# Attention A's output projection as seven block products for each pair of token tiles

## The chip, the cores and the metric

The kernel runs on one core of one Trainium2 chip. The metric is the device time of one execution in microseconds (us), as the median of several runs. All times of single instructions come from one profiled execution of the kernel before the change.

## The reference, cut to what matters

The program is one block of a transformer on an input of 2 sequences (B = 2) of T = 1024 tokens of C = 1024 features, all float32: attention A (32 heads of 32, causal, with ten adapter tokens), a feed-forward layer, attention B, and the same feed-forward layer again, each with a residual. The change concerns the last line of attention A and its residual:

```
y = einsum('bhqk,bhkd->bhqd', softmax(q k / sqrt(32), causal), v)
y = y + gating * einsum('bhqk,xhkd->bhqd', softmax(q ak / sqrt(C)), av)
y = y.transpose(0, 2, 1, 3).reshape(B, T, C)
x = x + einsum('btc,oc->bto', y, w_proj)
```

The last line is the output projection: a product of 2048 x 1024 by 1024 x 1024. Everything after it reads this x.

## The kernel before, in words

**Order of the work.** TensorE's (PE's) instructions are issued in program order. Attention A works in half-steps (`attend`, L454 to L533). In each of them PE multiplies scores twice: "s" scores (`sc`), from which VectorE (DVE) takes the row minimum (`pr_A`, `nmax_A`, L332), and transposed "t" scores (`st`), which ScalarE (ACT) turns into weights (`pt`, L503), and which then multiply the values (`y_A`, L413). Between the half-steps the `Filler` (L49 to L144) issues dense work from a queue of generators: the q, k and v projections of later heads, then the output projection. `fill.run` (L531) issues as much of it as an estimate of 1.7 ns for each column allows (`FILL_A`, L37); `fill.drain` issues what is left. `fill.chore` puts small DVE work in a list, one piece of which is issued after each fill step, and `fill.flush(key)` issues all pieces up to the last one with this key.

**Matmuls.** `mm` (L204) issues a product of a 128x128 block (`lhsT`, the stationary operand) and 128x512 columns (`rhs`) as one call at L207, or, directly behind attention's own matmuls, as four calls of 32 columns of the block each at L209. In float32 each call becomes two instructions in the trace. So one such product is 2 records at L207 or 8 at L209.

**The projections of q, k and v** (`seven`, L651) already use seven products of blocks in place of eight, in the form of Winograd. `factors` (L643) makes the combinations of the left blocks as chores, `combine` (L622) those of the right blocks, which go through DRAM and come back as `tt` tiles. The products land in two PSUM banks by turns, tags `ca` and `cb` (`block_bank`, L163), and DVE adds them up (L670 to L689).

**The output projection** (`proj_a`, L1020) is a plain product. For each of the 8 token tiles of a sequence, `yt` (128 features x 8 groups x 128 tokens) is fetched by eight DMAs of 64 KB from `yd`, where attention left its result. For each half of the 1024 output columns, eight products of 128x128 by 128x512 accumulate in one bank `op` (L1055), DVE adds the residual from `xp` (L1062), and SyncE's queue (SP) stores the sum to `x1` (L1063). So a tile takes 16 products, and a sequence 128. The weights `wp` are two tiles of 16 KB a partition (L1040) in the places of the normalized input.

Sequence 0's projection (`proj_a(0)`, L1009) is the last fill of attention A; what attention leaves of it is drained at L1304. Then the PSUM pool `psA` is closed, a new one with three `ps` banks is opened (L1306), and sequence 1's projection (`proj_a(1)`, L1310) runs with nothing beside it. It also issues the loads of the later weights (`each`, three in each tile). It is followed by the first feed-forward layer (`f1`), whose first tile is fetched and normalized within the last two tiles of the projection (`then.prepare`, L1049).

**SBUF.** Pool `big` holds `h16` (2 x 16 KB a partition: normalized input, later `wp`), `t4k` (3 x 4 KB: `yt`), `tt` (5 x 2 KB: `xp`). Pool `wkA` holds attention A's own tiles, among them the weights `wqk` (2 x 8 KB) and `wv` (8 KB); it is closed before the drain at L1304, and the later stages' weights take its place. In stage A the DMAs of SP are ordered by a scheduler; from L1308 on they go in program order.

**The adapter tokens.** For each group g of four heads of sequence 0, `adapter_parts` multiplies the adapter's tokens by the weights (L787), and `adapter_keys` (L792) and `adapter_values` (L798) sum the parts some fill steps later (L896, L929, L951). They share the only bank of tag `ps` with `shift_rows` and `adapter_scores`. `begin(b, g)` (L817) issues the parts and the left factors of the next group, for every group at the end of the previous one's projection (L838).

## Time and profile before

| what | value |
|---|---|
| time, median of 3 runs (lowest, highest) | 2494.17 us (2489.88, 2497.11) |
| the profiled execution | 2490.82 us, of which its span in the profile is 2489.1 us |
| output projection of sequence 0, between attention A's steps | 1205.8 to 1350 us |
| the rest of it and sequence 1's, alone on PE | 1350 to 1492 us |
| records of its matmuls | 338 at L207 and 696 at L209 |

Times inside an execution are counted from the start of the span. "Busy" is the time in which an engine worked on an instruction; matmuls overlap in their pipeline, so their durations add up to more than the time that they take, and the time from start to start is the better measure. "Idle before, releaser" names what an engine waited for before an instruction. SP's rows are the issuing of DMAs; a long SP row includes the time that SP waited for the tile to be ready or free.

### The profile page before, as it was taken

The numbers are of one execution on the slowest core, as the hardware profiler recorded it, in microseconds if no ns is written. First come the engines' busy times: TensorE is split into PE (matmuls) and PEld (weight loads), VectorE is DVE, ScalarE is ACT, GpSimd is POOL, SyncE is SP. The second block draws the span as 40 slices with busy tenths as digits, with TensorE's granted clock in tenths as the row PEclk, the third lists the DMA queues.
The fourth block names the chain that finished last, engine by engine and source line by source line (L and its number), as shares of the span: only waits on it lengthen the run. The fifth ranks groups of instructions, "written<-read, shape, count | busy, mean of one in ns | idle before, by whom it ended". The sixth has DMA issues, their size and how long they took to land.

```text
span 2489.1 us, 60414 instructions
## 1 busy us (share of the span) xinstructions
PE 2433.3 (98%) x25477; PEld 1101.6 (44%) x25477; DVE 1339.2 (54%) x4120; ACT 1090.0 (44%) x2085; POOL 499.1 (20%) x800
## 2 busy tenths in 40 slices
PE   7899999999999999999999999999999999999999
PEld 4434444455444545444433445574333653333344
DVE  7665665665656666665510114366554765654243
ACT  3346665665655666666631000012354535555200
POOL 1332322232423323322100001101000101111120
PEclk9999999999999999999999999999999999999999
DMA  6632322333333333333222541130110310212121
GB/s 214 208 90 80 104 86 84 100 90 103 125 93 104 93 105 95 91 90 117 86 69 81 190 158 64 43 102 26 41 37 27 137 35 35 86 43 94 40 97 42
DMA packets 142512, 224.34 MB, mean 90 GB/s; under 512 B 12832, under 2 KB 73376, under 8 KB 142240
## 3 DMA queue, kind: packets, MB, share of 16 engines
q1 hardware_dynamic: 142240, 220.48, 27.6%
q8 instruction: 199, 3.26, 0.5%
q14 instruction: 73, 0.60, 0.1%
HBM read 168.01 MB, written 52.43 MB: 89 GB/s over the span
## 4 chain that ended last, share of the span: by engine, by line
PE 88%; DVE 6%; issue 2%; DMA 2%; ACT 1%; POOL 1%; SPq 0%; DVEq 0%; ACTq 0%; POOLq 0%
PE fo_f L207 11%; PE st L391 9%; PE fo_f L209 7%; PE sc L319 7%; PE op L207 6%; PE y_A L413 5%; PE y L209 5%; PE z L209 3%; PE st L389 3%; PE op L209 3%; PE y_v L209 3%; PE x L209 3%; PE y_B L413 2%; PE bq L207 2%; DVE pr_A L332 2%
## 5 line engine op out<-in xcount | busy, mean ns | idle before, releaser
L503 ACT ACTIVATE pt<-st 128x1024 f32<-128x1024 f32 (+1 forms) x418 | 426.0, 1019 | 654.5 <-PE st L391 490.6
L340 ACT ACTIVATE pr_A<-pr_A,nmax_A 128x896 f32<-128x896 f32 (+7 forms) x512 | 389.9, 765 | 47.2 <-DVE nmax_A L332 46.5
L332 DVE CUSTOM_DVE_ANT_0 pr_A<-sc,mask 128x512 f32<-128x512 f32 (+3 forms) x512 | 251.1, 537 | 200.0 <-PE st L391 103.5
L319 PE MATMUL sc<-kT,qT 32*128 32x512 f32 (+3 forms) x1536 | 329.1, 525 | 4.4 <-DVE nmax_A L332 3.6
L391 PE MATMUL st<-qT,kT 32*128 32x512 f32 (+3 forms) x1536 | 307.2, 487 | 0.0
L207 PE MATMUL fo_f<-wb,xt_f 128*128 128x512 f32 x558 | 253.0, 596 | 0.4 <-ACT hwT_f L1153 0.4
L236 POOL TENSOR_TENSOR xf<-xf,b_base 128x256 f32<-128x256 f32 x128 | 89.3, 729 | 761.0 <-DVE xn_f L258 457.2
L332 DVE CUSTOM_DVE_ANT_0 pr_A<-sc,mask,part_A 128x512 f32<-128x512 f32 (+1 forms) x256 | 156.2, 647 | 147.3 <-PE sc L319 98.7
L209 PE MATMUL fo_f<-wb,xt_f 128*32 128x512 f32 x1864 | 223.6, 599 | 0.0
L398 POOL TENSOR_SCALAR_AFFINE_SELECT pt<-pt 128x256 f32<-128x256 f32 x256 | 104.5, 426 | 525.3 <-ACT pt L503 525.3
L340 ACT ACTIVATE pr_B<-pr_B,nmax_B 128x1024 f32<-128x1024 f32 x128 | 145.6, 1140 | 41.2 <-DVE nmax_B L332 41.2
L413 PE MATMUL y_A<-pt,v 128*32 128x512 f32 (+3 forms) x1536 | 157.9, 498 | 0.0
L207 PEld LDWEIGHTS fo_f<-wb,xt_f 128*128 128x128 f32 x558 | 103.4, 193 | 113.9 <-issue 113.3
L319 PE MATMUL sc<-kq,qk 32*128 32x512 f32 x512 | 144.3, 640 | 3.7 <-DVE nmax_B L332 3.3
L207 PE MATMUL op<-wp,yt 128*128 128x512 f32 x338 | 145.7, 592 | 0.0
L391 PE MATMUL st<-rows_B,kq 32*128 32x512 f32 x512 | 144.3, 640 | 0.0
L250 ACT ACTIVATE lv_f<-ve_f 128x1 f32<-128x1 f32 x32 | 6.5, 203 | 309.9 <-DVE ve_f L248 309.9
L391 PEld LDWEIGHTS st<-qT,kT 32*128 32x128 f32 x1536 | 134.0, 185 | 16.5 <-issue 11.4
L332 DVE CUSTOM_DVE_ANT_0 pr_B<-sc,mask,part_B 128x512 f32<-128x512 f32 x128 | 91.2, 747 | 79.8 <-PE sc L319 79.7
L389 PE MATMUL st<-rows_A,ones 3*128 3x512 bf16 (+3 forms) x768 | 127.8, 329 | 4.1 <-DVE nmax_A L332 4.1
L332 DVE CUSTOM_DVE_ANT_0 pr_B<-sc,mask 128x512 f32<-128x512 f32 x128 | 83.4, 687 | 75.9 <-PE sc L319 75.9
L319 PEld LDWEIGHTS sc<-kT,qT 32*128 32x128 f32 x1536 | 113.5, 184 | 18.6 <-issue 9.2
(274 smaller groups left out, 3648.2 us busy)
## 6 DMA issues: line engine op xcount, KB each, us to landing
tt<-td SPq DMA_DIRECT2D x252, 256.0 KB, 2.8
wqk<-in_w_attnT SPq DMA_DIRECT2D x32, 512.0 KB, 5.2
xf<-x SPq DMA_DIRECT2D x32, 512.0 KB, 3.3
xa<-in_x SPq DMA_DIRECT2D x16, 512.0 KB, 6.1
wv<-in_w_attnT SPq DMA_DIRECT2D x8, 1024.0 KB, 5.3
yd<-ys SPq DMA_DIRECT2D x32, 256.0 KB, 2.9
yt<-yd SPq DMA_DIRECT2D x128, 64.0 KB, 2.0
xp<-in_x SPq DMA_DIRECT2D x32, 256.0 KB, 2.9
```

Source lines behind the costliest of these rows:

```text
L207: return pe.matmul(out, lhsT=lhsT, rhs=rhs, start=start, stop=stop, skip_group_check=True)
L209: pe.matmul(out[i : i + 32], lhsT=lhsT[:, i : i + 32], rhs=rhs, start=start, stop=stop, skip_group_check=True)
L236: pool.tensor_add(dst[:, i : i + 2 * P], a[:, i : i + 2 * P], b[:, i : i + 2 * P])
L250: act.activation(lv, ve, AF.Ln)
L319: yield w * COL, lambda: pe.matmul(dst[:, o : o + w], lhsT=self.qt[rows, qc : qc + P], rhs=self.kt[rows, c0 : c0 + w], start=True, stop=True)
L332: minimum[0] = dve.tensor_tensor_reduce(pr[:, c0 : c0 + w], sc[:, i, o : o + w], m, -self.scale, BIG if c0 == 0 else self.part[:, col], AL ...
L340: tc.keep_in_program_order(act.activation(pr[:, :nk], pr[:, :nk], AF.Exp, bias=self.nmax[:, col], scale=-1.0, accum_out=self.sums[:, col]))
L389: yield w * COL / 4, lambda: pe.matmul(dst[:, o : o + w], lhsT=ones[three, :], rhs=self.rows[three, off : off + w], start=True, stop=False)
L391: yield w * COL, lambda: pe.matmul(dst[:, o : o + w], lhsT=self.kt[rows, kb * P : (kb + 1) * P], rhs=rhs, start=self.extra, stop=True)
L398: pool.affine_select(out=dg, in_=dg, compare_op=ALU.is_ge, fill=0.0, base=0, pattern=[[0, 2], [1, P]], channel_multiplier=-1)
L413: pe.matmul(self.y[32 * h : 32 * h + 32, off : off + w], lhsT=self.value(h, kb), rhs=pt[h // 2][:, h % 2, o : o + w], start=self.opens, st ...
L503: act.activation(pt[:, :, low_:wide_], st[:, :, low_:wide_], AF.Exp, scale=ts[0][0].scale)
```

## The change

Sequence by sequence, two token tiles form a pair. A pair's product is 256 tokens x 1024 by 1024 x 1024, seen as a 2x2 matrix of blocks (128 tokens x 512) times a 2x2 matrix of blocks (512 x 512). A plain product needs eight products of blocks, each of four matmuls (128x128 by 128x512). The change forms it from seven (`seven_added`), with sums and differences of blocks made by DVE (`left_factors` for the left, chores for the right). Pair 0 of sequence 0 is still computed plainly, while the three combinations of the weights are made; these lie in the places of `wqk` and `wv`, for which the two tags move to pool `big`. The last difference (`b12 - b11`) is made in place behind pair 0.

For this, sequence 0's projection is drained inside the pool `wkA`, in whose places (`sa`, `sv`, `qr`) the left factors and the sums lie, and sequence 1's projection runs in the PSUM pool of attention A, in the banks `ca` and `cb`, with a new small SBUF pool `pj`; the PSUM pool is exchanged behind it. A pair's `yt` tiles are fetched at the start of the pair before, its `xp` tiles behind the second product of the pair before, and each store is issued one addition late.

Three more things move in stage A: `begin(b, 1)` goes from the end of group 0's projection to the middle of it, ahead of `combine`; `adapter_keys` goes from fill step 4 to 12; and `adapter_values` from step 4 to 8, and for group 0 from the first pair of tiles to the second.

The diff, cut to its core:

```
         def v_load(b, g):
-            wv = wk.tile([P, NC, 2 * P], F32, tag="wv", name=f"wv{b}_{g}", bufs=1)
+            wv = big.tile([P, NC, 2 * P], F32, tag="wv", name=f"wv{b}_{g}", bufs=1)
...
-            if ng and nb < B:
+            if g and ng and nb < B:
                 yield from begin(nb, ng)
...
                     if b == 0:
                         yield from between
+                    yield from begin(b, 1)
                     combine(b)
...
-                    if i == 4 and b == 0:
+                    if i == 12 and b == 0:
                         yield adapter_keys(g)
...
-                    if i == 4 and b == 0 and g == e:
+                    if i == 8 and b == 0 and g == e:
                         yield adapter_values(g)
...
-                if n == 0 and t == 0:
+                if n == 0 and t == 2:
                     yield adapter_values(0)
...
+        def place(kind, i, shape, name):
+            if kind == "yt" or kind == "x":
+                return big.tile(shape, F32, tag={"yt": "t4k", "x": "tt"}[kind], name=name)
+            return wk.tile(shape, F32, tag={"s": "sa", "sum": ("sv", "sv", "qr")[i]}[kind], name=name, bufs=2)
+
+        fill.add(Dense(lambda: proj_a(0, big, wp, place)))
...
+    def seven_added(nm, left, right, ready, sums, x, ended):
+        s1, s2, s3 = sums
+        def product(i, dst, start=True, stop=True):
+            ready(i)
+            for k in range(4):
+                mm(dst, lhsT=left[i][:, k, :], rhs=right[i][:, k, :], start=start and k == 0, stop=stop and k == 3)
+                yield HF * COL
+        def added(i, s):
+            pin_add(x[i], s, x[i])
+            ended(i)
+        first = block_bank([P, HF], f"x_{nm}")
+        yield from product(1, first, stop=False)
+        act.copy(s1, first)
+        y = block_bank([P, HF], f"y6_{nm}", 1)
+        yield from product(6, y)
+        pin_add(s2, s1, y)
+        yield from product(2, first, start=False)
+        added(11, first)
+        y = block_bank([P, HF], f"y7_{nm}", 1)
+        yield from product(7, y)
+        pin_add(s1, s2, y)
+        pin_sub(left[3], left[3], left[6])
+        z = block_bank([P, HF], f"z_{nm}")
+        yield from product(5, z, stop=False)
+        pin_add(s3, s1, z)
+        added(22, s3)
+        y = block_bank([P, HF], f"y4_{nm}", 1)
+        yield from product(4, y)
+        pin_sub(s1, s1, y)
+        added(21, s1)
+        yield from product(3, z, start=False)
+        pin_add(s2, s2, z)
+        added(12, s2)
+        pair.rotate(1)
+
+    def left_factors(a, s1, s2, key):
+        for op, dst, x, y in ((pin_add, s1, a[21], a[22]), (pin_sub, s2, s1, a[11]), (pin_sub, a[21], a[11], a[21])):
+            fill.chore(key, lambda op=op, dst=dst, x=x, y=y: op(dst, x, y))
+        return {1: a[11], 2: a[12], 3: a[12], 4: a[22], 5: s1, 6: s2, 7: a[21]}
+
+    def proj_a(b, big, wp, tile_of, then=None, each=None):
...
+        def fetch(p):
+            for t in (2 * p + 1, 2 * p):
+                yts[t] = take("yt", [P, NG, P], f"yt{b}_{t}")
+                for g in range(NG):
+                    sp.dma_start(yts[t][:, g, :], yd[b, g][:, t * P : (t + 1) * P])
...
+        def store(t, n):
+            stores.append((x1[b, t][:, n * HF : (n + 1) * HF], xs.pop((t, n))))
+            if len(stores) > 1:
+                sp.dma_start(*stores.popleft())
...
+            for i, tag in ((3, "wqk"), (2, "wqk"), (4, "wv")):
+                wp["T", i] = big.tile([P, 4, HF], F32, tag=tag, name=f"wpt{i}")
...
+        for p in range(NT // 2):
+            if then is not None and p == NT // 2 - 1:
+                then.prepare()
+            if p + 1 < NT // 2:
+                fetch(p + 1)
+            if each is not None:
+                each()
+            if b == 0 and p == 0:
+                for c in range(4):
+                    for dst, op, x, y in ((7, pin_sub, b22, b12), (6, pin_add, right[7], b11), (4, pin_sub, right[6], b21)):
+                        fill.chore("wp", lambda c=c, dst=dst, op=op, x=x, y=y: op(right[dst][:, c], x[:, c], y[:, c]))
...
+                for c in range(4):
+                    fill.chore("wp1", lambda c=c: pin_sub(b12[:, c], b12[:, c], b11[:, c]))
+                continue
...
+            flush = {6: ("wp", nm), 5: ("wp1",)}
...
+            def ready(i):
+                for key in flush.get(i, ()):
+                    fill.flush(key)
+                if i == 2:
+                    while stores:
+                        sp.dma_start(*stores.popleft())
+                    if p + 1 < NT // 2:
+                        fetch_x(p + 1)
+                if i == 5:
+                    if each is not None:
+                        each()
+                    if then is not None and p == NT // 2 - 1:
+                        then.prepare()
...
-            big = PoolOf(bigp, {"h16": 2, "t4k": 3, "tt": RING})
+            big = PoolOf(bigp, {"h16": 2, "t4k": 3, "tt": RING, "wqk": 2, "wv": 1})
...
-            fill.drain()
-            psa.close()
-            ps = ctx.enter_context(tc.tile_pool(name="ps", bufs=3, space=bass.MemoryType.PSUM, reuse_waits="tile"))
+                fill.drain()
...
+            pj = PoolOf(own.enter_context(tc.tile_pool(name="pj", bufs=2, side="right", reuse_waits="tile")), {"sum": 3, "x": 3, "yt": 1})
...
+            fill.add(Dense(lambda: proj_a(1, big, wp, place, f1_0, lambda: load(3))))
             fill.drain()
             assert not loads
+            own.close()
+            psa.close()
+            ps = ctx.enter_context(tc.tile_pool(name="ps", bufs=3, space=bass.MemoryType.PSUM, reuse_waits="tile"))
```

More of the change, by code (lines that the diff above doesn't have):

```diff
@@ L224, in pin, with in_pieces, both, pin_sub @@
         return r
+    def in_pieces(op):
+        def both(dst, x, y):
+            for h in range(0, HF, 2 * P):
+                op(dst[:, h : h + 2 * P], x[:, h : h + 2 * P], y[:, h : h + 2 * P])
+        return both
+    def pin_sub(*a):
+        pin(dve.tensor_sub(*a))
+    def pin_add(*a):
+        pin(dve.tensor_add(*a))
     def evac(dst, src):
@@ L603, in stage_a @@
         streams = {}
-        def in_pieces(op):
-            def both(dst, x, y):
-                for h in range(0, HF, 2 * P):
-                    op(dst[:, h : h + 2 * P], x[:, h : h + 2 * P], y[:, h : h + 2 * P])
-            return both
-        def pin_sub(*a):
-            pin(dve.tensor_sub(*a))
-        def pin_add(*a):
-            pin(dve.tensor_add(*a))
         def made(ts, b, i, c, op, x, y):
@@ L703, in qk_load @@
         def qk_load(b, g):
-            wqk = wk.tile([P, NC, 2, P], F32, tag="wqk", name=f"wqk{b}_{g}", bufs=2)
+            wqk = big.tile([P, NC, 2, P], F32, tag="wqk", name=f"wqk{b}_{g}", bufs=2)
             for s in range(2):
@@ L1007, in stage_a @@
                          ("unit", f"A{old // NG}_{old % NG}_1") if old >= 0 else None)
-        wp = []
-        fill.add(Dense(lambda: proj_a(0, big, wp)))
+        wp = {}
+        def place(kind, i, shape, name):
[3 more added lines that the diff above has]
+        fill.add(Dense(lambda: proj_a(0, big, wp, place)))
         attend([make(b, g, n) for b in range(B) for g in range(NG) for n in range(2)], FILL_A, late)
@@ L1017, in ahead_of @@
                 yield r
-    def proj_a(b, big, wp, then=None, each=None):
-        yts, xs = {}, {}
-        def fetch(t):
-            if t >= NT:
-                return
-            yts[t] = big.tile([P, NG, P], F32, tag="t4k", name=f"yt{b}_{t}")
-            for g in range(NG):
-                sp.dma_start(yts[t][:, g, :], yd[b, g][:, t * P : (t + 1) * P])
-        def fetch_x(t):
-            if t >= NT:
-                return
-            for n in range(2):
-                xs[t, n] = big.tile([P, HF], F32, tag="tt", name=f"xp{b}_{t}_{n}")
+    def seven_added(nm, left, right, ready, sums, x, ended):
[32 more added lines that the diff above has]
+        pair.rotate(1)
@@ new lines, in left_factors, with take, fetch_x @@
+    def left_factors(a, s1, s2, key):
[3 more added lines that the diff above has]
+    def proj_a(b, big, wp, tile_of, then=None, each=None):
+        yts, xs, stores = {}, {}, deque()
+        count = {"yt": 0, "x": 0}
+        def take(kind, shape, name):
+            count[kind] += 1
+            return tile_of(kind, count[kind] - 1, shape, name)
+        def fetch(p):
[3 more added lines that the diff above has]
+                    sp.dma_start(yts[t][:, g, :], yd[b, g][:, t * P : (t + 1) * P])
+        def fetch_x(p):
+            for t, n in ((2 * p, 0), (2 * p + 1, 1), (2 * p + 1, 0), (2 * p, 1)):
+                xs[t, n] = take("x", [P, HF], f"xp{b}_{t}_{n}")
@@ L1036, in fetch_x @@
                 sp.dma_start(xs[t, n], d["x"][b, t * P : (t + 1) * P, n * HF : (n + 1) * HF])
+        def store(t, n):
+            stores.append((x1[b, t][:, n * HF : (n + 1) * HF], xs.pop((t, n))))
+            if len(stores) > 1:
+                sp.dma_start(*stores.popleft())
         if not wp:
             for i in range(2):
-                wp.append(big.tile([P, 4, C], F32, tag="h16", name=f"wp{i}"))
+                wp[i] = big.tile([P, 4, C], F32, tag="h16", name=f"wp{i}")
                 for g in range(4):
@@ L1042, in proj_a @@
                     sp.dma_start(wp[i][:, g, :], d["w_projT"][(4 * i + g) * P : (4 * i + g + 1) * P, :])
+            for i, tag in ((3, "wqk"), (2, "wqk"), (4, "wv")):
+                wp["T", i] = big.tile([P, 4, HF], F32, tag=tag, name=f"wpt{i}")
+        b11, b12, b21, b22 = (wp[i][:, :, n * HF : (n + 1) * HF] for i in range(2) for n in range(2))
+        right = {1: b11, 2: b21, 3: b22, 4: wp["T", 4], 5: b12, 6: wp["T", 2], 7: wp["T", 3]}
         fetch(0)
         fetch_x(0)
-        fetch(1)
@@ L1046, in proj_a @@
         yield READY
-        for t in range(NT):
-            if then is not None and t >= NT - 2:
+        for p in range(NT // 2):
+            if then is not None and p == NT // 2 - 1:
                 then.prepare()
-            fetch(t + 2)
-            yt = yts.pop(t)
-            for n in range(2):
-                op = (next_bank if b == 0 else bank)([P, HF], f"op{b}_{t}_{n}")
-                for g in range(NG):
-                    mm(op, lhsT=yt[:, g, :], rhs=wp[g // 4][:, g % 4, n * HF : (n + 1) * HF], start=(g == 0), stop=(g == NG - 1))
-                    yield HF * COL
-                if n == 0:
-                    fetch_x(t + 1)
-                    if each is not None:
-                        each(t)
-                x = xs.pop((t, n))
-                dve.tensor_add(x, op, x)
-                sp.dma_start(x1[b, t][:, n * HF : (n + 1) * HF], x)
+            if p + 1 < NT // 2:
[6 more added lines that the diff above has]
+                        fill.chore("wp", lambda c=c, dst=dst, op=op, x=x, y=y: op(right[dst][:, c], x[:, c], y[:, c]))
+                for t in (1, 0):
+                    yt = yts.pop(t)
+                    for n in range(2):
+                        op = next_bank([P, HF], f"op{b}_{t}_{n}")
+                        for g in range(NG):
+                            mm(op, lhsT=yt[:, g, :], rhs=wp[g // 4][:, g % 4, n * HF : (n + 1) * HF],
+                               start=(g == 0), stop=(g == NG - 1))
+                            yield HF * COL
+                        x = xs[t, n]
+                        dve.tensor_add(x, op, x)
+                        store(t, n)
+                    if t == 1:
+                        fetch_x(p + 1)
+                for c in range(4):
+                    fill.chore("wp1", lambda c=c: pin_sub(b12[:, c], b12[:, c], b11[:, c]))
+                continue
+            nm = f"p{b}_{p}"
+            a = {10 * i + j: yts.pop(2 * p + i - 1)[:, 4 * j - 4 : 4 * j] if j == 2 else yts[2 * p + i - 1][:, 4 * j - 4 : 4 * j]
+                 for i in (1, 2) for j in (1, 2)}
+            left = left_factors(a, *(tile_of("s", i, [P, 4, P], f"s{i}_{nm}") for i in range(2)), nm)
+            flush = {6: ("wp", nm), 5: ("wp1",)}
+            ends = {11: (2 * p, 0), 12: (2 * p, 1), 21: (2 * p + 1, 0), 22: (2 * p + 1, 1)}
+            def ready(i):
[5 more added lines that the diff above has]
+                    if p + 1 < NT // 2:
+                        fetch_x(p + 1)
+                if i == 5:
+                    if each is not None:
+                        each()
+                    if then is not None and p == NT // 2 - 1:
+                        then.prepare()
+            yield from seven_added(nm, left, right, ready, [tile_of("sum", i, [P, HF], f"sum{i}_{nm}") for i in range(3)],
+                                   {i: xs[at] for i, at in ends.items()}, lambda i: store(*ends[i]))
@@ L1064, in proj_a @@
+        sp.dma_start(*stores.popleft())
         yield ("proj", b)
@@ L1303, in tile_model @@
                     wp = stage_a(PoolOf(wk, {"pr": 6, "qk": 6, "pt": 4}), big)
-            fill.drain()
-            psa.close()
-            ps = ctx.enter_context(tc.tile_pool(name="ps", bufs=3, space=bass.MemoryType.PSUM, reuse_waits="tile"))
+                fill.drain()
             order = ctx.enter_context(ExitStack())
             order.enter_context(tc.manual_schedule(engines={mybir.EngineType.SP}))
+            own = ExitStack()
             f1_0 = Dense(lambda: f1(0))
-            proj = Dense(lambda: proj_a(1, big, wp, f1_0, lambda t: load(3)))
-            proj.prepare()
-            fill.add(proj)
             wts = ctx.enter_context(tc.tile_pool(name="wts", bufs=1, side="right", reuse_waits="tile"))
@@ L1343, in f2, with place @@
                            lambda t: ("x3", b, t) in fill.done)
+            pj = PoolOf(own.enter_context(tc.tile_pool(name="pj", bufs=2, side="right", reuse_waits="tile")), {"sum": 3, "x": 3, "yt": 1})
+            def place(kind, i, shape, name):
+                if kind == "yt" and i % 4 < 3 or kind == "x" and i % 8 < RING:
+                    return big.tile(shape, F32, tag={"yt": "t4k", "x": "tt"}[kind], name=name)
+                return pj.tile(shape, F32, tag=kind, name=name)
+            fill.add(Dense(lambda: proj_a(1, big, wp, place, f1_0, lambda: load(3))))
             fill.drain()
             assert not loads
+            own.close()
+            psa.close()
+            ps = ctx.enter_context(tc.tile_pool(name="ps", bufs=3, space=bass.MemoryType.PSUM, reuse_waits="tile"))
         wb = PoolOf(ctx.enter_context(tc.tile_pool(name="wkB", bufs=2, side="left", reuse_waits="tile")), {"pr": 6, "pt": 4})
```

## The prediction, made before the changed kernel ran

> **What bounds the kernel.** I read the page's busy shares and chain first, then PE's waits, then the windows and the order of time around the projection.

> ```profile
> PE 2433.3 (98%) x25477; PEld 1101.6 (44%) x25477; DVE 1339.2 (54%) x4120; ACT 1090.0 (44%) x2085; POOL 499.1 (20%) x800
> ...
> PE 88%; DVE 6%; issue 2%; DMA 2%; ACT 1%; POOL 1%; SPq 0%; DVEq 0%; ACTq 0%; POOLq 0%
> ...
> L207 PE MATMUL op<-wp,yt 128*128 128x512 f32 x338 | 145.7, 592 | 0.0
> ```

> PE is busy in 98% of the span, and the chain that ended last is PE for 88% of it. The last row is the projection's: no idle time before it. The windows say the same for its stage (window, length, then busy time and records of PE, PEld, DVE, ACT, POOL, granted clock, DMA share, GB/s):

> ```profile
> 1225.00:1235.00 10.00, 10.00 (x92) 3.29 (x91) 5.22 (x18) 5.08 (x8) 0.77 (x2) 1.00 0.37 120
> ...
> 1300.00:1350.00 50.00, 50.00 (x420) 14.85 (x418) 3.46 (x5) 12.76 (x13) 2.34 (x6) 1.00 0.22 69
> 1350.00:1382.00 32.00, 32.00 (x78) 14.17 (x75) 2.76 (x4) 0.00 (x0) 0.00 (x0) 1.00 0.30 98
> 1382.00:1492.00 110.00, 110.00 (x258) 48.60 (x257) 14.65 (x25) 0.41 (x2) 2.77 (x4) 1.00 0.58 187
> ```

> PE never stops between 1205 and 1492 us, and DVE has almost nothing to do behind 1250. So a matmul taken out here is time taken out, if no new wait comes in.

> **What is removed.** The order of time gives the price of one matmul:

> ```profile
> 1350.26 141.89 PE L207 MATMUL op<-wp,yt 128*128 128x512 f32 x330
> ```

> 330 records are 165 products (two records each) in 141.89 us: 0.86 us for one. The row's 592 ns is the length of one overlapping record and isn't the price. A pair needs 28 products for 32; seven of the eight pairs change: 28 products fewer, 28 x 0.86 = **24.1 us**. In attention's part a group of 32 records (four products) takes 3.55 us from 1346.71 to 1350.26, and one of 16 takes 1.83 (1317.60 to 1319.43): again 0.86 a product, so the three pairs of sequence 0 save 12 x 0.86 = 10.3 us and the four of sequence 1 save 16 x 0.86 = 13.8.

> Is the part inside attention paid out? Of the 165 products behind attention's last step 128 belong to sequence 1, so 37 of sequence 0's are drained at the end. With 12 fewer, 25 remain; attention's steps don't run out of fill, and the 10.3 us come off the drain.

> [...]

> **What is added on DVE.** Each changed pair has 3 left factors and 10 additions, so 91 in seven pairs, with 16 for the weights and 4 for the plain pair 111, where there were 32. The same additions of the q and k projections show their length:

> ```profile
> L670 DVE TENSOR_TENSOR kT<-qT,y x14: 679/682/686, 120.1 to 1149.9; 128x512 f32<-128x512 f32 x14
> ...
> L612 DVE TENSOR_TENSOR s<-s,wqk x14: 671/687/1219, 112.8 to 1110.5; 128x512 f32<-128x512 f32 x14
> ...
> L665 ACT COPY qT<-x x14: 560/569/586, 112.6 to 1142.5; 128x512 f32<-128x512 f32 x14
> ```

> (Minimum, median, maximum in ns.) 79 more x 0.69 = 54 us on DVE, and 7 ACT copies of 0.57. A pair brings 13 x 0.69 = 9.0 us of DVE beside 24.1 us of PE. What hides each is the product between: a bank is read behind its product, and needed again one product, 4 x 0.86 = 3.4 us, later; reading takes 0.69 us. I cost them at 0. Without that cover, 0.69 and some 0.25 from matmul to addition (as 1491.99 to 1492.19 in DVE's last `xp`) would stand in the open for each of 49 products: the slow rival below.

> The 12 weight chores come while attention's minima still run. From 1205 to 1245 DVE is busy 19.2 of 40 us; 12 x 0.69 = 8.3 more fit, and DVE has 1.3 to 3.9 us idle before most minima there. The first also waits for the second half of `wp`, issued from 1201.75 to 1204.2 and landing 6.1 us later, about 1208, while the minima behind it wait in DVE's queue and PE's next scores wait for them. From 0 to 8.3 us; I take 1, because the idle time before the minima is larger than one chore.

> **What is moved among DMAs.** Bytes and counts stay: 128 fetches of 64 KB, 32 of `xp`, 32 stores, 18 weights. But sequence 0 has three `yt` places for pairs of two. The second tile of a pair (2p, whose left half is the first factor used) takes the place of tile 2p-1, which is last read by product 4; only product 3 (3.4 us) lies between. An issue takes 0.43 us and lands in 2.0:

> ```profile
> yt<-yd SPq DMA_DIRECT2D x128, 64.0 KB, 2.0
> ...
> 1356.17 2.81 SPq L1029 DMA_DIRECT2D yt<-yd  x6
> ```

> The first block is there 0.2 + 0.43 + 2.0 = 2.6 us behind product 4, and each next 0.43 later while PE needs one each 0.86: in time. If the wait is for the whole tile, it is 0.2 + 8 x 0.43 + 2.0 = 5.6, so 2.2 us late, at three boundaries (into pairs 2 and 3 and into sequence 1) 6.6. Taken: 1.5. From sequence 1's second pair on, four `yt` and eight `xp` places leave a whole pair of 24 us. Behind SP's waiting fetches stand `xp` loads and stores, needed 10 us later or not at all; SP held by a store would add its longest row here, 7.2, to each boundary, 29 in all with the 2.2: kept as the far end.

> At sequence 1's end, f1's first tile is normalized behind product 7 instead of within the last two tiles. The chain took 3.7 us (1479.06 to 1482.7); three products, 10.3 us, lie behind it. Nothing. The exchange of the PSUM pool now falls there too; in the drain at 1382 it left no gap. At most the last addition, 0.7; taken 0.

> **What is moved in attention.** PE's waits that these edits touch:

> ```profile
> PE avp L800 <- DVE ae L755: 2.7, 1, 2.7
> ...
> PE akp L209 <- DVE ae L755: 2.2, 1, 2.2
> PE y L209 <- DVE s L612: 2.0, 1, 2.0
> ...
> PE akp L207 <- DVE awTA L229: 0.8, 1, 0.8
> PE st_A L209 <- ACT parts_k L231: 0.6, 1, 0.6
> ```

> (Sum, times, longest.) The adapter's sums wait for the bank `ps`, which DVE still reads; some steps later it is free. The first `y` waited for left factors that stood behind `combine`'s chores, and now stand ahead. With 0.2 more of `akp` these are 8.5 us. DVE then is late next: at 96 and 102 us the scores wait 1.6 and 2.1 us for its minima, and part of a gain turns into that. From 0 to 8.5, and as the moved `ps` users can meet another reader, down to -3 (the longest wait of this kind). I take 3.5, less than half.

> **The sum.** 24.1 + 3.5 - 1 - 1.5 = 25.1 us. On the profiled execution 2490.8 - 25.1 = 2465.7; on the median of the runs, which is 3.4 above it, 2494.2 - 25.1 = **2469 us**. With the ends of the small terms the gain is 24.1 + 8.5 = 32.6 at best and 24.1 - 3 - 8.3 - 6.6 = 6.2 at worst without SP held up.

> **The rivals.**

> *Waits for the banks (slower).* Products take turns in two banks; `op` of sequence 1 had three. If every product waited for the addition before it, 49 x 0.94 = 46 us would stand against 24.1: 2494 + 22 = 2516. From 0.49 us a product on the change loses. Against it: q, k and v have run 21 such rounds, 147 products, beside the far busier DVE of attention, and PE's waits show for their `x`, `y`, `z` only the 2.0 us above.

> *Late tiles.* The boundaries of sequence 0 cost 6.6 to 29 us instead of 1.5, or the chores 8.3: the gain is about 10, 2484; at the far end nothing, or 4 us slower. For it: the places are three for four. Against it: blocks arrive singly, and in the profile PE's start on a fresh `yt` shows no gap. [...]

> *Only sequence 1 pays.* If attention's last steps, not the fill, set its end, 13.8 us come off: 2480. The 37 products behind it speak against that.

> **Chances.** The forecast (2461 to 2478) 0.68; more, since all waits of attention go, 0.05; only sequence 1 or late tiles with a gain of 8 to 16 us 0.13; gain used up within 0.3% (7.5 us, about what a measurement of this kernel can tell from no change) 0.08; slower, by bank waits or SP held, 0.06. So faster 0.86, same 0.08, slower 0.06. Below 2460 and above 2484 I leave 0.04 and 0.15; the runs themselves spread over 7 us, which is inside.

> **What will show it.** The projection's products should be 228 instead of 256, sequence 1's 112 without a break in some 96.5 us, with 0.86 each. PE's waits should have no row of more than 1 us on the additions, and under 3 us on `yt`; `avp`, `akp` and the first `y` should be gone from them. DVE grows by 54 us. A PE row that waits for DVE's additions in each pair would make the forecast wrong, and so would gaps of several us before products 1 of pairs 2 and 3.

## The result, and the profile after

| | median (lowest, highest), us | ratio to before |
|---|---|---|
| before | 2492.03 (2485.8, 2497.11), 4 runs | |
| changed | 2463.03 (2460.57, 2465.15), 4 runs | 0.9884 [0.9858, 0.991] |

The kernel is 29.0 us faster. Timed again beside each other, on two chips, the two kernels lay 25.5 and 27.4 us apart (e1_again and e12_changed below). The changed kernel's profiled execution took 2463.84 us, with a span of 2462.1. The two profiled spans divide as follows. The projection's stage is counted from its first matmul to the first transposition of `f1`. Where products are counted or priced, as in the prediction, a product is one of 128x128 by 128x512 (two records at L207); products numbered 1 to 7 are those of a pair, of four such products each.

| span | attention, until the projection starts | projection | all that follows | whole |
|---|---|---|---|---|
| before | 1205.8 | 286.2 | 997.1 | 2489.1 |
| changed | 1207.6 | 262.2 | 992.3 | 2462.1 |
| gain | -1.8 | 24.0 | 4.8 | 27.0 |

Busy times and chain on the page of the changed kernel, the answer to the first lines shown of before:

```profile
PE 2406.4 (98%) x25433; PEld 1091.6 (44%) x25433; DVE 1389.0 (56%) x4199; ACT 1093.6 (44%) x2092; POOL 497.1 (20%) x800
...
PE 87%; DVE 6%; issue 2%; DMA 1%; ACT 1%; POOL 1%; SPq 0%; DVEq 0%; ACTq 0%
```

PE has 26.9 us less of busy time and DVE 49.8 more, and PE is busy in 98% of the span as before. DVE's work has not come into the chain. The windows of the projection's stage (columns as before):

```profile
1207.60:1230.00 22.40, 22.40 (x252) 9.14 (x250) 18.45 (x53) 12.01 (x25) 4.86 (x10) 1.00 0.24 87
...
1300.00:1352.10 52.10, 52.10 (x440) 15.28 (x428) 12.15 (x18) 13.51 (x15) 3.11 (x8) 1.00 0.26 83
1352.10:1469.80 117.70, 117.70 (x278) 52.12 (x275) 44.06 (x69) 3.33 (x7) 6.45 (x7) 1.00 0.61 200
```

PE's busy time equals the length of each window. The weight chores fall into the first one: DVE is busy 18.45 of 22.40 us there, and PE still has no gap. The order of time on PE (start, us, instruction, in brackets a wait and its releaser) shows the unbroken row:

```profile
1370.24 3.60 PE L207 MATMUL z_p<-wp,yt 128*128 128x512 f32 x8
1373.67 3.60 PE L207 MATMUL x_p<-wp,yt 128*128 128x512 f32 x8
1377.10 3.60 PE L207 MATMUL y_p<-wpt,s_p 128*128 128x512 f32 x8
...
1466.37 3.60 PE L207 MATMUL z_p<-wp,yt 128*128 128x512 f32 x8
1469.80 0.60 PE L213 MATMUL xt_f<-ident,xn_f 128*128 128x128 f32 x4
1470.75 0.66 PE L213 MATMUL xt_f<-ident,xn_f 128*128 128x128 f32 x4 [0.34 <-DVE sum_p L236]
```

Every 3.43 us four products start. There are 228 of them, as predicted. Sequence 1 runs from 1373.67 to 1469.80: 112 products in 96.1 us, 0.858 each. The only wait on an addition in the whole stage is the 0.34 us at its end. Of attention's waits on PE (sum, times, longest) the following touch the moved steps:

```profile
PE st_A L209 <- DVE ae L755: 3.5, 6, 1.5
...
PE akp L207 <- DVE awTA L241: 3.0, 2, 1.5
PE avp L800 <- DVE ae L755: 2.8, 2, 1.4
...
PE xt_a L213 <- ACT xnT L243: 2.4, 1, 2.4
...
PE akp L209 <- DVE ae L755: 1.6, 1, 1.6
...
PE xt_a L213 <- DVE awTA L241: 1.3, 1, 1.3
PE akp L207 <- ACT awTA L243: 1.1, 1, 1.1
```

The first `y` has lost its wait for `s`. `avp` has kept its 2.7 us, and `akp` has grown from 3.2 us to 5.7.

### The profile page after: what moved, and what is told of

Its sections match the earlier page's. It is cut to its first block, busy times and chain, and to the rows that moved or that the text cites. A ratio compares the mean times of both kernels' runs of the same rounds, so it can differ in the third digit from the quotient of the medians.

```text
span 2462.1 us, 60457 instructions
## 1 busy us (share of the span) xinstructions
PE 2406.4 (98%) x25433; PEld 1091.6 (44%) x25433; DVE 1389.0 (56%) x4199; ACT 1093.6 (44%) x2092; POOL 497.1 (20%) x800
## 4 chain that ended last, share of the span: by engine, by line
PE 87%; DVE 6%; issue 2%; DMA 1%; ACT 1%; POOL 1%; SPq 0%; DVEq 0%; ACTq 0%
PE fo_f L207 11%; PE st L403 9%; PE fo_f L209 7%; PE sc L331 7%; PE y_A L425 5%; PE y L209 5%; PE z L209 3%; PE st L401 3%; PE x L209 3%; PE y_v L209 3%; PE y_B L425 2%; PE y_p L207 2%; DVE pr_A L344 2%; PE bq L207 2%; PE x_v L209 2%
## 5 line engine op out<-in xcount | busy, mean ns | idle before, releaser
L207 PE MATMUL fo_f<-wb,xt_f 128*128 128x512 f32 x558 | 251.3, 593 | 0.4 <-ACT hwT_f L1253 0.4
L209 PE MATMUL fo_f<-wb,xt_f 128*32 128x512 f32 x1864 | 221.9, 595 | 0.0
L207 PEld LDWEIGHTS fo_f<-wb,xt_f 128*128 128x128 f32 x558 | 102.9, 192 | 112.7 <-issue 112.2
L1240 DVE TENSOR_TENSOR xf<-fo_f,xf 128x512 f32<-128x512 f32 x64 | 44.2, 691 | 139.2 <-PE fo_f L207 113.1
L401 PEld LDWEIGHTS <-ones 3*128 3x128 bf16 x768 | 36.8, 91 | 193.8 <-issue 186.4
```

The source lines that it names most:

```text
L207: return pe.matmul(out, lhsT=lhsT, rhs=rhs, start=start, stop=stop, skip_group_check=True)
L209: pe.matmul(out[i : i + 32], lhsT=lhsT[:, i : i + 32], rhs=rhs, start=start, stop=stop, skip_group_check=True)
L401: yield w * COL / 4, lambda: pe.matmul(dst[:, o : o + w], lhsT=ones[three, :], rhs=self.rows[three, off : off + w], start=True, stop=False)
L1240: dve.tensor_add(x[:, cols], ops[n], x[:, cols])
```

## The experiments

The main table gives each profiled execution by stage. "Half" counts windows of 3.41 us in which the granted clock was 0.5, in attention, projection and rest. A half-speed window behind the last matmul is left out. Each of the others costs up to 1.7 us, an estimate: half of its length, at half the clock. "Start less half" is the start of the projection with 1.7 us taken off for each one in attention.

| kernel | timed median | before on that chip | start | projection | rest | half | start less half |
|---|---|---|---|---|---|---|---|
| before | | | 1205.8 | 286.2 | 997.1 | 7, 0, 2 | 1193.9 |
| changed | 2463.03 | 2492.03 | 1207.6 | 262.2 | 992.3 | 6, 0, 0 | 1197.4 |
| e1_again | 2463.96 | 2489.47 | 1207.9 | 262.2 | 992.3 | 5, 0, 0 | 1199.4 |
| e2_proj_only | 2460.98 | 2489.47 | 1201.3 | 262.2 | 992.9 | 4, 0, 0 | 1194.5 |
| e3_moves_only | 2493.31 | 2489.47 | 1206.8 | 286.2 | 1000.3 | 5, 0, 3 | 1198.3 |
| e4_seq0_plain | 2474.74 | 2489.47 | 1205.1 | 272.5 | 992.5 | 4, 0, 0 | 1198.3 |
| e5_uncovered | 2478.41 | 2490.58 | 1207.4 | 275.1 | 995.5 | 5, 0, 1 | 1198.9 |
| e6_late_fetch | 2486.76 | 2490.58 | 1205.2 | 284.7 | 993.7 | 4, 5, 0 | 1198.4 |
| e7_begin_only | 2455.52 | 2490.58 | 1202.1 | 262.2 | 991.8 | 6, 0, 0 | 1191.9 |
| e8_pair0 | 2466.22 | 2490.58 | 1206.8 | 264.9 | 992.8 | 7, 1, 1 | 1194.9 |
| e9_begin_again | 2457.04 | 2489.65 | 1198.3 | 262.2 | 992.6 | 3, 0, 0 | 1193.2 |
| e10_keys_late | 2460.49 | 2489.65 | 1203.4 | 262.2 | 993.6 | 5, 0, 1 | 1194.9 |
| e11_values_late | 2458.09 | 2489.65 | 1200.8 | 262.2 | 994.2 | 4, 0, 1 | 1194.0 |
| e12_changed | 2462.28 | 2489.65 | 1208.1 | 262.2 | 991.4 | 6, 0, 0 | 1197.9 |

### The projection and the moves, each alone

e1_again is the changed kernel beside the next three on one chip.

> The changed kernel once more, beside the kernel before on the same chip. Theory: the 28 products left out are worth 24.1 us and nothing else of the change is worth anything, so 24 us below before, with what the two kernels' half-clock windows add or take (each of 3.4 us costs 1.7). Rival: the moves in attention are worth 3.5 us, so 27 to 29.

Ratio 0.9895 [0.9879, 0.991]. e2_proj_only puts the five moved places in attention back:

```
-            if g and ng and nb < B:
+            if ng and nb < B:
-                    yield from begin(b, 1)
-                    if i == 12 and b == 0:
+                    if i == 4 and b == 0:
-                    if i == 8 and b == 0 and g == e:
+                    if i == 4 and b == 0 and g == e:
-                if n == 0 and t == 2:
+                if n == 0 and t == 0:
```

> The changed kernel with the three moves in attention (begin, adapter_keys, adapter_values) put back. Theory, that the moves are worth nothing: same as the changed kernel within 2 us, PE's waits on the banks as before the change. Rival, that they are worth 3.5 us: 3 to 4 us slower than the changed kernel.

Ratio 0.9886 [0.9873, 0.99]. e3_moves_only makes these five edits, the other way round, in the kernel before:

> The kernel before with the three moves alone, the projection as it was. Theory: within 2 us of before, akp's waits grow from 3.2 to 5.7 us and the first y's 2.0 goes. Rival: 3.5 us faster than before.

Ratio 1.0014 [1.0006, 1.0023], 3.8 us slower than before. e2_proj_only gains 28.5 us and e1_again 25.5 on the same chip. So the change of the projection alone brings all of the gain, and the moves take time. The projection's length does not depend on them (262.2 and 262.2; 286.2 and 286.2). That e2_proj_only gains more than the 24.0 us of its projection is taken up below, under what follows the projection.

### Does the part inside attention pay?

e4_seq0_plain computes all of sequence 0 plainly (as pair 0) and leaves the seven products to sequence 1:

```
-            if b == 0 and p == 0:
+            if b == 0:
...
-                for t in (1, 0):
+                for t in (2 * p + 1, 2 * p):
```

> The changed kernel with all four pairs of sequence 0 computed plainly: 12 products more. Theory, that a product inside attention is paid out like one outside: 10.3 us slower than the changed kernel, and the number of products left for the drain behind attention rises from 25 to 37. Rival, that only sequence 1 pays: as fast as the changed kernel within 2 us.

It is 10.8 us slower than e1_again on the same chip, and its projection is 10.3 us longer (272.5 and 262.2); 12 products at 0.858 are 10.3. Behind attention's last step 37 of sequence 0's products are left again, as the theory had it. So the part inside attention pays in full, off the drain.

### The cover of the banks

e5_uncovered issues product 7 ahead of product 2, so that products meet a bank whose sum was just begun:

```
-        yield from product(2, first, start=False)
-        added(11, first)
         y = block_bank([P, HF], f"y7_{nm}", 1)
         yield from product(7, y)
+        yield from product(2, first, start=False)
+        added(11, first)
```

> The changed kernel with product 7 directly behind product 6 and product 2 behind it, so that in each pair product 7 and product 5 start in a bank whose addition has just begun: 14 waits without cover. Rival theory of the banks, with 0.69 for the addition and 0.25 to start it: about 0.94 us for each of the 8 in sequence 1 and the 2 in sequence 0's drained pair, the other four partly covered by attention's own matmuls, so 9 to 13 us slower than the changed kernel. If it is within 2 us of the changed kernel, the cover wasn't needed.

Ratio 0.9953 [0.994, 0.9965]; the projection grows by 12.9 us, within the 9 to 13 of the theory. Its order of time on PE, and its waits:

```profile
1381.07 3.60 PE L207 MATMUL y_p<-wpt,s_p 128*128 128x512 f32 x8
1385.51 3.70 PE L207 MATMUL y_p<-wpt,yt 128*128 128x512 f32 x8 [0.85 <-DVE sum_p L236]
1389.05 3.60 PE L207 MATMUL x_p<-wp,yt 128*128 128x512 f32 x8
1393.43 3.70 PE L207 MATMUL z_p<-wp,s_p 128*128 128x512 f32 x8 [0.78 <-DVE xp L236]
```

```profile
PE y_p L207 <- DVE sum_p L236: 4.2, 5, 0.9
PE z_p L207 <- DVE xp L236: 3.9, 5, 0.8
...
PE y_p L209 <- DVE sum_p L236: 0.9, 1, 0.9
...
PE z_p L209 <- DVE xp L236: 0.8, 1, 0.8
```

From start to start the first waiting round takes 4.44 us for 3.43 and the second 4.38, and the product after a wait takes another 0.11. Twelve waits are seen, so a bank without cover costs 12.9 / 12 = 1.08 us. The order of the products in `seven_added` avoids just that.

### A fetch that comes late

e6_late_fetch issues a pair's `yt` fetches in sequence 1 at the start of their own pair, not of the one before:

```
-            if p + 1 < NT // 2:
+            if p + 1 < NT // 2 and b == 0:
                 fetch(p + 1)
+            if p and b == 1:
+                fetch(p)
```

> The changed kernel with sequence 1's pairs 1 to 3 fetched at their own start instead of one pair earlier. SP comes to these fetches behind a store that waits for product 4's additions, some 1.7 us behind product 4, and the first block needed is the ninth of 0.45 us each and lands 2.05 later: 4.4 us late at each of three boundaries, 13 us slower than the changed kernel. [...] If the price of a late tile is what the small-term ends of the prediction had (2.2 each), 7.

Ratio 0.9992 [0.9981, 1.0004]: nearly the whole gain is gone, at three boundaries. PE's waits, then the order of time on PE, then the windows around the first boundary:

```profile
PE x_p L207 <- DMA yt<-yd: 15.1, 3, 6.5
```

```profile
1399.68 5.37 PE L207 MATMUL x_p<-wp,yt 128*128 128x512 f32 x8 [4.30 <-DMA yt<-yd]
1404.89 3.60 PE L207 MATMUL y_p<-wpt,s_p 128*128 128x512 f32 x8
...
1462.99 6.48 PE L207 MATMUL x_p<-wp,yt 128*128 128x512 f32 x8 [6.49 <-DMA yt<-yd]
1469.30 3.60 PE L207 MATMUL y_p<-wpt,s_p 128*128 128x512 f32 x8
```

```profile
1396.90:1400.30 3.40, 0.61 (x2) 0.41 (x3) 0.69 (x1) 0.00 (x0) 0.00 (x0) 1.00 0.49 136
1400.30:1403.70 3.40, 3.40 (x6) 1.39 (x5) 1.29 (x2) 0.00 (x0) 0.00 (x0) 0.51 0.32 86
```

The waits are 15.1 us. The first four products behind each wait take 5.21 to 6.31 us for 3.43, 7.0 us more in all: the clock column falls to 0.51 in the window after the nearly idle one, and there are five half-speed windows in the stage. 15.1 + 7.0 = 22.1 of the 22.6 us by which the projection grows. That is more than the 13 expected: the last wait was 6.5 us and not 4.4, and the slowed products cost 7.0 besides.

### Which of the moves costs

e7_begin_only leaves the left factors' start moved and puts back the adapter's three steps only (the last three edits of e2_proj_only's diff).

> The changed kernel with the adapter's sums (adapter_keys, adapter_values) back at their old steps, and begin still moved. If the adapter's steps are what costs the 3.4 us of the moves: as fast as the kernel with all three moves put back, 2 to 4 us below the changed kernel. If begin is: same as the changed kernel.

Ratio 0.9862 [0.9847, 0.9877]. It was run again beside the changed kernel, with kernels in which only the keys' step (`i == 12`), or only the two values' steps (`i == 8`, `t == 2`), are late:

> As in e7: the changed kernel with the adapter's three steps back at their old places and only the left factors' start moved. Theory (the later adapter steps cost time, the earlier left factors gain some): 8 us below e12 on this chip, the projection starting about 5 us earlier (1202 against 1207). Rival (e7's 8 us belonged to the other chip, as the kernels were never timed side by side): within 3 us of e12.

> Of the adapter's steps only the keys' is late (i == 12); both edits of the values are back at their old places. Theory (the keys' step is what costs: the akp waits went from 3.2 to 5.7 us, and a half-clock window of 1.7 us stands behind each of two of them): as e12, 6 to 8 us above e9. Rival (the values' steps cost it): within 2 us of e9. If they share it: about 4 above e9.

> Of the adapter's steps only the values' are late (i == 8, t == 2); the keys' step is back at its old place. Theory (the keys' step is what costs, since the wait avp <- ae is 2.7 us before and after): within 2 us of e9. Rival (the values' steps cost it): as e12, 6 to 8 us above e9. If they share it: about 4 above e9.

> The changed kernel once more, beside the three others on one chip. Theory and rival alike: 26 to 30 us below the kernel before, projection 262 us long, starting at 1207 to 1208.

Ratios: 0.9862 [0.9843, 0.9881], 0.9875 [0.9854, 0.9896], 0.9866 [0.9851, 0.9882] and 0.9889 [0.9871, 0.9906]. e9 is 5.2 us faster than the changed kernel on the same chip, and no run of the one (2452.6 to 2459.29) lies within those of the other (2460.75 to 2467.1). The 8 us expected were too many, but the sign repeats: the version that moves only the left factors beats both kernels. Between e9 and e12, the keys' step makes 3.4 us and the values' steps 1.1. The runs of e10 and e11 overlap with each other and with those of e9; the profiles decide better. In e10_keys_late these rows of PE's waits are those of the changed kernel:

```profile
PE akp L207 <- DVE awTA L241: 3.0, 2, 1.5
...
PE akp L209 <- DVE ae L755: 1.6, 1, 1.6
PE xt_a L213 <- DVE awTA L241: 1.3, 1, 1.3
...
PE akp L207 <- ACT awTA L243: 1.1, 1, 1.1
```

and in e9_begin_again the first and the last are shorter, and the third is missing:

```profile
PE akp L209 <- DVE ae L755: 2.0, 1, 2.0
...
PE akp L209 <- DVE rows_A L241: 1.2, 1, 1.2
...
PE akp L207 <- DVE awTA L241: 0.8, 1, 0.8
...
PE akp L207 <- ACT awTA L243: 0.2, 1, 0.2
```

7.0 us against 4.2. At step 12 PE finds DVE and ACT still at the copies `awTA`, and waits for them. That this place is bad for that reason is read from these rows; no other place was tried. With the values late (e11), `avp` waits 2.8 us in two places for 2.7 in one, and `xt_a` 2.4 us for ACT's `xnT` in place of 1.3 for DVE's.

With the half-speed windows taken off, the starts agree well: 1193.9 to 1194.9 where all places are the old ones (before, e2, e8), 1191.9 and 1193.2 where only `begin` is moved, 1194.9 and 1194.0 with the keys' or the values' steps late besides, and 1197.4 to 1199.4 in all seven profiles with all moves. So the left factors' move gains some 2 us, the late keys take back 2.3 and the late values 1.5, and both together nearly 6 (means 1192.6 and 1198.4). The numbers for the keys and for the values rest on one profile each. The four runs of each kernel, by an estimate that takes the span times the mean granted clock of each run, give 2446.2 us with only `begin` moved (e9), 2450.9 with the keys late (e10), 2447.2 with the values late (e11) and 2452.8 with all (e12): 4.7 for the keys, 1.0 for the values, 6.6 for both. That the keys cost more than the values holds by both; the sizes do not agree closely.

### Pair 0 by seven products too

e8_pair0 is e2_proj_only with pair 0 of sequence 0 also formed from seven, so that 4 more products go and 16 weight sums are due within its first products:

```
-            flush = {6: ("wp", nm), 5: ("wp1",)}
+            flush = {6: ("wp", nm), 5: ("wp1",), 4: ("wp4",)}
```

(and the plain branch for pair 0 is removed, its chores put under the keys `wp`, `wp1`, `wp4`).

> A version meant to beat both kernels: the moves put back, and pair 0 of sequence 0 by seven products too, with its weights' sums as chores ahead (first those for products 6 and 7, then the others). Theory: 4 products less, 3.4 us below the kernel with the moves put back, less up to 3 us of waits for the weights' sums on DVE: 0 to 3.4 below it. Rival: the burst of 16 sums delays attention's minima by more than 3.4, so slower than it.

Ratio 0.9904 [0.9891, 0.9918]. The projection takes 264.9 us, where 4 products less would make 262.2 - 3.4 = 258.7 (before rounding). PE's wait and the windows of that place:

```profile
PE y_p L209 <- DVE s_p L233: 4.3, 1, 4.3
```

```profile
1214.90:1218.50 3.60, 0.33 (x4) 0.16 (x8) 3.60 (x8) 0.46 (x1) 0.71 (x1) 0.98 0.00 0
1218.50:1221.90 3.40, 3.40 (x36) 1.10 (x32) 1.42 (x3) 0.00 (x0) 0.00 (x0) 0.51 0.00 0
```

DVE is busy for the whole of the first window, while PE works for 0.33 us of it; in the next one PE's granted clock is 0.51. 4.3 + 1.7 = 6.0 of the 6.2 us that are missing. So the version gains less than e2_proj_only, as the rival had it, but what waits is product 6, for a left factor that stands behind the weights' sums on DVE; the wait seen isn't one for attention's minima. The plain pair 0 is what covers the weight sums.

## Why the prediction was right, point by point

The time of 2463.0 us lies inside the range of 2461 to 2478. The gain is 29.0 us for the 25.1 predicted, or 26.7 by the means of more runs (below). The main term and its mechanism were right. Of the small terms the moves had the wrong sign, and a term that the sum didn't have, PE's clock, made up for it; that part was luck.

**The products removed.** 24.1 us predicted, 24.0 measured as the difference of the two projections; in e2_proj_only, too, 24.0. 25 products stand behind attention's last step, as predicted: (1373.67 - 1352.1) / 0.858 = 25.1. The price from the row, 0.86, was the right one: 0.858 measured in sequence 1.

**DVE.** 79 more instructions as counted, and 49.8 us instead of 54. They cost nothing on PE, because of the cover that was named; e5 shows the price without it, 1.08 us for 0.94 predicted. By that price the rival's 49 waits would have cost 53 us, an estimate.

**The weight chores.** Taken 1 us of 0 to 8.3. No gap is seen in the first 22.4 us, so 0 here. e8 shows the far end: 16 sums with less ahead of them cost 6.0 us.

**Late tiles.** Taken 1.5 us of 0 to 6.6. PE has no wait for `yt`. SP's order of time in the changed kernel, at the boundary into sequence 1, shows the issues that wait for the freed place:

```profile
1370.43 1.27 SPq L1088 DMA_DIRECT2D yt<-yd  x3
1371.88 0.32 SPq L1098 DMA_DIRECT2D x<-xp  x1
1372.24 2.35 SPq L1088 DMA_DIRECT2D yt<-yd  x5
```

They start as product 4 ends, 0.19 us behind the start of product 3 (1370.24), as the prediction had it, and follow each other at 0.4 to 0.5 us, with one store between. The first block lands at 1372.27 and the last at 1376.26. PE starts on this tile at 1373.67 without a wait, so it needs the single blocks and not the whole tile, and SP isn't held by the store: 0 us, then. The mechanism exists: e6 pays 4.3 to 6.5 us at a boundary, and for the slowed products 7.0 at the three besides. Two numbers of the prediction don't follow from its own terms: three times 7.2 + 2.2 is 28 and not 29, and a gain of about 10 would need the late tiles and the chores at their ends, and no gain from the moves.

**The start of f1 and the PSUM exchange.** 0.34 us of wait for 0 taken (0.7 at most).

**The moves in attention: this step failed.** Taken was a gain of 3.5 us, less than half of the 8.5 us of waits named. Alone, the moves cost 3.8 us (e3). The largest of the small terms thus had the wrong sign. The step took the waits of `avp` and `akp` as due to their place in the fill; `avp` keeps its wait at the later place, `akp`'s grew, and only `y`'s went. The range named, -3 to 8.5, was passed at its lower end: 3.8 us by e3's time, 4.0 by the means of the starts less half (1194.4 with the old places, 1198.4 with all moves). Span times granted clock, as above, gives 4.7 from e2 to e1 and 5.9 from before to e3. The two profiled spans show only 1.8 of it, since before happened to have one half-speed window more.

**What follows the projection.** Taken as unchanged; it is 4.8 us shorter, and so the wrong sign of the moves didn't show in the sum. Behind the projection each engine has the same instructions in the same order in both kernels, but for 12 of PE's 7288 records. 3.4 of the 4.8 us are two half-speed windows that before has and the changed kernel hasn't.

This is no chance of two profiles: the granted clock of before is 0.992 to 0.996 in 39 runs on three chips (mean 0.9942), that of the changed kernel 0.996 or 0.997 in 12 runs (mean 0.9965). By the means, the span falls by 26.7 us (2488.1 to 2461.4), and span times clock, the time at full clock, by 20.9 (2473.7 to 2452.8). So some 21 us are the products less the moves, and some 6 the clock, for which the prediction had no term. This is an estimate, as the clock is given to three digits (0.001 is 2.5 us) and span times clock counts PE as at work in all of a half-speed window, where it worked for 1.1 to 3.4 us of 3.41. Which windows are spared differs from profile to profile: behind the projection the two kernels with the plain one have 2 and 3, and the twelve with the new one 0 or 1. Why the new projection leaves fewer was not tested.

Of the remaining 1.4 of the 4.8 us a part is one of PE's waits, in before and then in the changed kernel:

```profile
PE sc L319 <- DVE nmax_B L332: 3.3, 3, 1.4
```

```profile
PE sc L331 <- DVE nmax_B L344: 1.0, 3, 0.4
```

Less 1.7 for each window, the rest is 993.7 us in before and 991.1 to 993.8 in the kernels with the new projection. Why DVE's minima of attention B come later in before wasn't settled: DVE's longest wait for a DMA of `xb` is 3.9 us there against 2.7.

## What to carry to other kernels

Where PE is the bound and never stops in a stage, a product taken out is worth its start-to-start time in that stage (0.858 us here), and the sums that replace it were free here, with one product of a pair (3.43 us) between a bank's last product and its next use; without that, each cost about 1.08 us (e5_uncovered). A wait in the profile is no promise: before moving a step to avoid it, look at who uses its bank or engine at the new place, and try each move by itself, since two of the three moves here lost more than the third gained. Compare the granted clock too: about 6 of the 27 us between these two kernels come from it, by the estimate above. Put sums for weights that are due at once behind work that doesn't need them: without that they cost 6.0 us in e8_pair0.

## What the runs showed of the hardware that was not expected

In the traces of before and of the changed kernel the granted clock is 1.00 or 0.50. Up to the last matmul every stretch at 0.50 is 3.413 us long, but for one of 6.827 in before, and all half-speed windows of a profile start whole multiples of 3.413 us apart (in the changed kernel 58.72, 99.67, 147.46, 167.94, 253.28, 621.91: 12, 14, 6, 25 and 108 windows). The whole span can so be divided into windows of 3.413 us, counted from these starts. Two of them in the changed kernel, each with the one behind it:

```profile
164.53:167.94 3.41, 1.31 (x35) 0.31 (x21) 3.41 (x16) 1.65 (x6) 0.00 (x0) 1.00 0.00 0
167.94:171.35 3.41, 3.40 (x32) 1.00 (x31) 0.83 (x2) 0.00 (x0) 2.97 (x5) 0.50 0.07 8
225.97:229.38 3.41, 2.18 (x28) 0.92 (x24) 1.99 (x6) 2.53 (x6) 1.23 (x3) 1.00 0.27 77
229.38:232.79 3.41, 3.41 (x44) 1.11 (x38) 1.04 (x4) 2.79 (x6) 0.41 (x1) 1.00 0.02 5
```

By these counts a wait of 2.1 us would cost 3.8 us where it falls in one window and leaves 1.3 us of work there (2.1 and a half-speed window of 1.7), and 2.1 where it lies across two; this is an estimate, and no run shifted a wait against the windows. That also bears on the scatter: the four runs of e9 took 2452.6 and 2454.79 us at a mean granted clock of 0.998, and 2459.28 and 2459.29 at 0.995. 0.003 of the clock is 7.4 us of such a run (5 to 10 with the rounding of the clock), and the two pairs lie 5.6 us apart.
